# Attention in six half rounds a step, 256-column products between them, and sigmoids behind attention

## The chip, the cores and the metric

One core of a Trainium2 chip runs one program. The metric is the device time of one execution in microseconds; the median of three runs is quoted. TensorE (PE) multiplies, VectorE (DVE) and ScalarE (ACT) work on its results in PSUM banks of 512 f32 columns, GpSimd (POOL) works on SBUF, and SyncE (SP) issues most DMAs. Every engine runs its own instructions in their written order and waits on semaphores for the others.

## The reference

An AdaLN block on x (8 batch rows of 512 tokens, width 256), all in f32:

```python
mod = (_silu(c) @ wmod).reshape(8, 6, 1, -1)        # sa, ca, ga, sb, cb, gb; ga and gb kept away from 0
h = _layernorm(x) * (1 + ca) + sa
x = x + ga * attention(h)
h = _layernorm(x) * (1 + cb) + sb
x = x + gb * ffn(h)
```

`attention` has 16 heads over a latent of 64: `logits = q_lat @ latent_k / 8`, causal, softmax, times `latent_v`, up, then `Wout`. `ffn` is a mixture of 16 experts, each of which takes the 512 best of the 4096 tokens by `sigmoid(h @ gate_w.T)`, with gate, up and down products, plus a shared expert of width 512 (`silu(h @ shg) * (h @ shu)`, then `shd`) that all tokens pass.

## The kernel before

**Attention** goes in 32 steps; step n is batch row b and group g of four heads, `divmod(n, 4)`, written (b,g) here. In the body of the loop at L849 three steps overlap:

- For the next step, `scores` (L603) writes rows of query tile i against the keys that causality leaves (128(i+1) columns) into a bank `sc_ps`, and `maxima` (L611) reduces it on VectorE to the row maxima `mx`, one reduction with its accumulator's read for each head j and tile i.
- For this step, `fold` (L625) transposes the maxima on TensorE, and VectorE subtracts them from the query strips q (L630). Then `scores_t` (L632) writes the transposed scores of key tile c (512 - 128c columns) into a bank `st_ps`, and `exps` (L640) makes p on ScalarE; on every second head GpSimd masks the diagonal block (L650).
- For the last step, `context` (L660) multiplies v by p into `po`, 16 matmuls of four tiles c; ScalarE copies it to `oT`, and `gather` sends it off by DMA. For every second step the sums' reciprocal (`invert`), a store and a fetch through DRAM (`fetch`) and a multiplication on VectorE (`divide`, L698) follow.

The 128 x 128 array holds sixteen 32 x 32 matmuls at once; `quarters` (L555) issues four for one head, so that two heads of the next step and two of this one fill it. This is a half round: all with the same number of columns, 512, 384, 256 or 128. A step has eight (k = 0 to 7), two of each size. Banks come from rotating tags: three for `sc_ps` (and fold's transposes), three for `st_ps`, and two, tag m, for everything else, context included.

Between half rounds stand the **slots**: `plan(n)` lists the other work of a step with a price in us of TensorE (0 for what others do), and `laid_out` deals it to nine slots by a table of VectorE's time for each half round. The other work: transposes, latents, queries, keys and values of rows to come (`turn_h` L483, `latents` L493, `query` L581, `key` L596, `value` L502), `residual` (L537) of the row before, the second norm and the gate's scores (`Second`), and the shared expert of the rows behind (`Shared`, L272; two rows within attention, "early", the others after it). A product of 512 columns with its two weight halves is two pieces of one matmul each. Written order of a step: slot 0, fold, context of tiles 0 and 1, half round 0, context of tiles 2 and 3, slot 1, half round 1, slot 2, and so on to slot 8.

`sigmoid` (L439) makes the gate's sigmoids of two batch rows by a polynomial on VectorE, in four parts, and stores them with two DMAs. Three of the four calls are in the plan of steps (3,0), (5,0) and (7,0), in slots 1, 3, 5 and 7.

**After attention** a tail (L900 to L921) ends the last row; after each of its parts `work()` issues two pieces of the late shared products. A search on VectorE (L967) finds each expert's threshold in 30 rounds, again with `work()` in between, and the experts follow, about half of the time, which the change does not touch.

Of the kernel before, what the change touches and what calls it, by code (L numbers as in the profile page):

```python
# [50 lines left out]
def block_kernel(ctx: ExitStack, tc: tile.TileContext, a: dict, out: bass.AP):  # L51
# [219 lines left out]

    class Shared:  # L272
# [10 lines left out]
        def product(self, ps, w, f, c):  # L283
            nc.tensor.matmul(
                ps,
                lhsT=w[:, c, f * P : (f + 1) * P],
                rhs=h2T[:, c, self.b * T : (self.b + 1) * T],
                start=(c == 0),
                stop=(c == KC - 1),
            )  # L290

        def gate(self, f, c):
            if c == 0:
                if f == 0:
                    flush()
                    self.begin()
                self.pg = bank("pg2") if self.early else bank_s("pg2")
            self.product(self.pg, shg, f, c)
            if c < KC - 1:
                return  # L300
# [8 lines left out]
        def up(self, f, c):  # L309
            if c == 0:  # L310
                self.pu = bank("pu2") if self.early else bank_t("pu2")
            self.product(self.pu, shu, f, c)
            if c < KC - 1:
                return
# [7 lines left out]
        def down(self, i, h):  # L322
            i2, ii = divmod(i, 2)
            if h == 0:
# [3 lines left out]
            for f in range(h * NS // 2, (h + 1) * NS // 2):  # L328
                nc.tensor.matmul(
                    self.py[:, ii, :],  # L330
                    lhsT=self.mid[:, f, i * P : (i + 1) * P],
                    rhs=shd[:, f, :],
                    start=(f == 0),
                    stop=(f == NS - 1),
                )
            if ii == 1 and h == 1:
# [18 lines left out]
        def units(self):  # L355

            for f in range(NS):
                for c in range(KC):
                    yield c == 0, lambda f=f, c=c: self.gate(f, c)
                for c in range(KC):  # L360
                    yield c == 0, lambda f=f, c=c: self.up(f, c)
            for i in range(TT):
                for h in range(2):
                    yield i % 2 == 0 or h == 0, lambda i=i, h=h: self.down(i, h)
# [103 lines left out]
    class Row:  # L468
# [24 lines left out]
        def latents(self, cs=range(KC)):  # L493
            for c in cs:
                if c == 0:
                    self.lat = ap.tile([P, T], F32, name="lat", bufs=1)
                    self.pl = bank("pl")
                nc.tensor.matmul(self.pl, lhsT=wkv[:, c, :], rhs=self.hT[:, c, :], start=(c == 0), stop=(c == KC - 1))
                if c == KC - 1:
                    nc.scalar.copy(self.lat, self.pl)  # L500

        def value(self, i2):  # L502
            pv = bank("pv").rearrange("p (i h w) -> p i h w", h=H, w=DH)
            for ii in range(2):
                i = 2 * i2 + ii
                nc.tensor.matmul(
                    pv[:, ii, :, :].rearrange("p h w -> p (h w)"),
# [5 lines left out]
            for ii in range(2):  # L513
                nc.scalar.copy(v[:, 2 * i2 + ii, :, 0:HS:2], pv[:, ii, :, :])
# [22 lines left out]
        def residual(self, i):  # L537
            i2, ii = divmod(i, 2)
            if ii == 0:
                self.py = bank("py").rearrange("p (i d) -> p i d", d=D)  # L540
            for c in range(KC):
# [7 lines left out]
            if ii == 1:  # L549
# [10 lines left out]
    class Step:  # L560
# [20 lines left out]
        def query(self, cs=range(KC)):  # L581

            for c in cs:
                if c == 0:
                    self.pq = bank("pq")
                nc.tensor.matmul(
                    self.pq,
                    lhsT=wq[:, c, self.g * P // 2 : (self.g + 2) * P // 2],
                    rhs=self.r.hT[:, c, :],
# [3 lines left out]
                if c == KC - 1:  # L593
                    self.spread(self.pq, "q8", q_strips)

        def key(self):  # L596
            pk = bank("pk")
            nc.tensor.matmul(
                pk, lhsT=wlat[0:L, self.g * P // 2 : (self.g + 2) * P // 2], rhs=self.r.lat[0:L, :], start=True, stop=True
            )  # L600
            self.spread(pk, "k8", k_strips)

        def scores(self, j, i):  # L603

            n = (i + 1) * P
            sc_ps = bank_t("sc_ps") if self.n == 0 and j % 2 else bank_s("sc_ps")
            k = self.strip(j)
            quarters(sc_ps[:, 0:n], self.q[k, i * P : (i + 1) * P], self.k[k, 0:n])
            return sc_ps

        def maxima(self, sc_ps, j, i):  # L611
# [3 lines left out]
                sc_ps[:, 0:n],  # L615
                sc_ps[:, 0:n],
# [15 lines left out]
        def scores_t(self, j, c):  # L632

            n = T - c * P
            st_ps = bank_t("st_ps")
            k = self.strip(j)
            quarters(st_ps[:, 0:n], self.k[k, c * P : (c + 1) * P], self.q[k, c * P : T])
            return st_ps

        def exps(self, st_ps, j, c):  # L640
            n = T - c * P
            if c == 0 and j == 0:
                self.p = {}
            if j == 0:
                self.p[c] = ap.tile([P, NG, n], F32, name=f"p{c}", tag=f"p{c}", bufs=1)
            nc.scalar.activation(self.p[c][:, j, :], st_ps[:, 0:n], AF.Exp, scale=SCALE)  # L646
            if j % 2 == 1:
# [74 lines left out]
    SLOTS = 2 * TT + 1  # L722

    def plan(n):
# [4 lines left out]
        def add(slot, us, fn):  # L729
            todo.append((slot, us, fn))  # L730

        if n < 0:
            add(1, 1.8, modulate_t)
            for c in range(KC):
                add(2 + 2 * c, 0.86, lambda c=c: steps[2].query([c]))
            return todo
        if n == 0:
            for i in range(TT):
                add(i, 0.0, lambda i=i: stats(TT + i, mv))
# [4 lines left out]
        if g == (1 if b > 0 else 2) and b + 1 < B:  # L744
            for c in range(KC):
                add(0, 0.5, lambda c=c: rows[b + 1].turn_h(c))
            for c in range(KC):
                add(0, 0.86, lambda c=c: rows[b + 1].latents([c]))
        if n + 2 < len(steps) and n % 2 == 0:
            for c in range(KC):  # L750
# [616 lines left out]
```

## Time and profile before

| | us |
|---|---|
| median of 3 runs (1375.0 to 1378.51) | 1375.79 |
| the profiled execution | 1378.61 |
| its span, first to last instruction | 1376.9 |
| first fold to last fold (31 steps of attention) | 30.95 to 552.34 |
| last step and tail | 552.34 to 621.03 |
| search, placing, first fetch | 621.03 to 708 |
| experts | 708 to 1376.9 |

In the lines of the profile, times are us from the span's start unless marked ns; "x" is a count of records. A matmul in f32 is two records, each with a weight load (PEld). A matmul's end is modelled, and matmuls are pipelined, so the distance from one start to the next tells more than a length. What stands in brackets is the engine's idle time ahead of the instruction and whoever ended it. A row of a table by stretch has the stretch, its length, each engine's busy time, the granted TensorE clock as a share of full speed, and the DMA engines' share and rate. A slot's work is known by its line: L284 shared gate and up, L329 shared down, L488 `turn_h`, L498 latents, L506 values, L542 residual, L586 queries, L598 keys, L398 `turn`.

### The profile page before, as it was taken

The numbers are of one execution on the slowest core, as the hardware profiler recorded it, in microseconds if no ns is written. First come the engines' busy times: TensorE is split into PE (matmuls) and PEld (weight loads), VectorE is DVE, ScalarE is ACT, GpSimd is POOL, SyncE is SP. The second block draws the span as 40 slices with busy tenths as digits, with TensorE's granted clock in tenths as the row PEclk, the third lists the DMA queues.
The fourth block names the chain that finished last, engine by engine and source line by source line (L and its number), as shares of the span: only waits on it lengthen the run. The fifth ranks groups of instructions, "written<-read, shape, count | busy, mean of one in ns | idle before, by whom it ended". The sixth has DMA issues, their size and how long they took to land. (4 is left out here: it accounts for less than half of the span.)

```text
span 1376.9 us, 34203 instructions
## 1 busy us (share of the span) xinstructions
PE 1334.4 (97%) x14002; PEld 864.3 (63%) x14002; DVE 886.8 (64%) x2342; ACT 483.7 (35%) x1125; POOL 544.5 (40%) x629
## 2 busy tenths in 40 slices
PE   9999999989999899999999999999999999999997
PEld 4444334434434334465555888888888888888885
DVE  5756567656665667246664767777676777777653
ACT  1655555555455454411111322223332222333221
POOL 4552525252615232310013543454554345555331
PEclk9999999999999999999999999999999999999999
DMA  7122212221231221217022354444445444444511
GB/s 237 43 71 47 74 41 59 53 72 38 64 65 48 51 65 48 59 42 227 20 66 93 82 143 130 120 116 127 124 97 143 127 124 109 135 114 107 143 16 16
DMA packets 84349, 122.42 MB, mean 89 GB/s; under 512 B 14937, under 2 KB 61657, under 8 KB 84193
## 3 DMA queue, kind: packets, MB, share of 16 engines
q1 hardware_dynamic: 69120, 93.76, 22.7%
q0 software_dynamic: 14336, 25.70, 9.7%
q8 instruction: 110, 1.80, 0.5%
q10 hardware_dynamic: 736, 0.79, 0.2%
q14 instruction: 47, 0.38, 0.1%
HBM read 90.33 MB, written 21.51 MB: 81 GB/s over the span
## 5 line engine op out<-in xcount | busy, mean ns | idle before, releaser
L614 DVE CUSTOM_DVE_ANT_0 sc_ps<-sc_ps,causal 128x256 f32<-128x256 f32 (+3 forms) x512 | 240.9, 514 | 125.0 <-PE sc_ps L558 72.2
L646 ACT ACTIVATE p<-st_ps 128x256 f32<-128x256 f32 (+3 forms) x512 | 198.6, 439 | 212.1 <-PE st_ps L558 208.2
L558 PE MATMUL st_ps<-q,k 32*32 32x512 f32 (+3 forms) x4096 | 240.5, 443 | 2.4 <-ACT p L646 2.0
L558 PE MATMUL sc_ps<-k,q 32*32 32x512 f32 (+3 forms) x4096 | 236.8, 442 | 2.9 <-DMA k<-k 1.1
L1195 PE MATMUL epy<-dw,emid 128*128 128x256 f32 x1024 | 236.0, 382 | 1.8 <-DVE emid L1165 0.8
L650 POOL TENSOR_SCALAR_AFFINE_SELECT p<-p 128x256 f32<-128x256 f32 x256 | 105.2, 414 | 324.4 <-ACT p L646 323.5
L1220 POOL DMA_INDIRECT out<-eo,idx x64 | 102.1, 1596 | 315.9 <-DVE eo L1212 190.8
L1195 PEld LDWEIGHTS epy<-dw,emid 128*128 128x128 f32 x1024 | 192.0, 190 | 38.3 <-DVE emid L1165 12.9
L1142 ACT COPY c<-eu 128x256 f32<-128x256 f32 x120 | 44.7, 373 | 400.4 <-issue 224.9
L1125 PE MATMUL eu<-xsum,wsum 128*128 128x256 f32 x720 | 176.1, 381 | 0.0
L558 PEld LDWEIGHTS sc_ps<-k,q 32*32 32x32 f32 x4096 | 71.4, 103 | 142.4 <-DVE mx L614 89.2
L1125 PEld LDWEIGHTS eu<-xsum,wsum 128*128 128x128 f32 x720 | 135.7, 190 | 17.9
L1125 PE MATMUL eu<-xT,gu 128*128 128x256 f32 x480 | 142.8, 379 | 0.0
L1082 POOL DMA_INDIRECT rows<-rows_d,idx x64 | 62.3, 974 | 135.8 <-DVE mid L320 94.5
L1144 DVE TENSOR_TENSOR c<-eu,c 128x256 f32<-128x256 f32 x120 | 51.0, 425 | 100.8 <-ACT c L1143 98.4
L1165 DVE SCALAR_TENSOR_TENSOR emid<-eu,ub,esg 128x512 f32<-128x512 f32 x128 | 90.1, 743 | 28.8 <-ACT esg L1161 19.4
L1161 ACT ACTIVATE esg<-eu,gbias 128x512 f32<-128x512 f32 x128 | 81.5, 684 | 58.3 <-PE eu L1125 33.6
L1125 PEld LDWEIGHTS eu<-xT,gu 128*128 128x128 f32 x480 | 91.2, 190 | 12.4
L1145 DVE TENSOR_TENSOR eu<-eu,c 128x512 f32<-128x512 f32 x120 | 83.9, 699 | 4.1
L665 PE MATMUL po<-p,v 128*32 128x512 f32 (+3 forms) x1024 | 84.1, 447 | 0.6 <-DVE sg L305 0.5
L1042 DVE TENSOR_TENSOR at_q<-pos_lo,iota 128x1024 bf16<-128x1024 f32 x64 | 75.2, 1217 | 0.0
L614 DVE DVE_READ_ACCUMULATOR2_ANT mx<- 128x1 f32 x512 | 72.5, 142 | 0.0
(187 smaller groups left out, 1875.6 us busy)
## 6 DMA issues: line engine op xcount, KB each, us to landing
gu<-in_gw SPq DMA_DIRECT2D x16, 1024.0 KB
gu<-in_up SPq DMA_DIRECT2D x16, 1024.0 KB
dw<-in_dw SPq DMA_DIRECT2D x16, 1024.0 KB
q<-q SPq DMA_DIRECT2D x32, 128.0 KB
rows_d<-mod_d SPq DMA_DIRECT2D x8, 512.0 KB
rows_d<-row SPq DMA_DIRECT2D x8, 512.0 KB
out<-ysb SPq DMA_DIRECT2D x16, 256.0 KB
k<-k SPq DMA_DIRECT2D x30, 128.0 KB
```

Of the source, the lines that this page charges most:

```text
L558: nc.tensor.matmul(out[w : w + HS, :], lhsT=lhsT[:, w : w + HS], rhs=rhs, start=True, stop=True)
L614: nc.vector.tensor_tensor_reduce(sc_ps[:, 0:n], sc_ps[:, 0:n], causal[:, T - n : T], 1.0, -3.0e38, ALU.add, ALU.max, self.m[:, i, o : o + 1],)
L646: nc.scalar.activation(self.p[c][:, j, :], st_ps[:, 0:n], AF.Exp, scale=SCALE)
L650: nc.gpsimd.affine_select(out=p, in_=p, pattern=[[0, 2], [1, P]], compare_op=ALU.is_ge, fill=0.0, base=0, channel_multiplier=-1,)
L665: nc.tensor.matmul(self.po[self.strip(j), c * P : T], lhsT=v[:, c, self.g * NG + j, :], rhs=self.p[c][:, j, :], start=(c == 0), stop=(c == ...
L1042: nc.vector.tensor_tensor(self.at_q[:, n, :], pos_lo[:, e, n].unsqueeze(2).to_broadcast([P, QT, P]), iota.unsqueeze(1).to_broadcast([P, QT ...
L1125: nc.tensor.matmul(self.u[:, q, :], lhsT=w, rhs=x, start=start, stop=True, skip_group_check=not start)
L1145: nc.vector.tensor_tensor(u[:, 1:3, :], u[:, 1:3, :], c3.unsqueeze(1).to_broadcast([P, 2, HC]), ALU.add)
L1161: nc.scalar.activation(sg, pg, AF.Silu, bias=gbias[:, e, f : f + 1])
L1165: nc.vector.scalar_tensor_tensor(mid[:, f, :], pu, ub[:, e, f : f + 1], sg, ALU.add, ALU.mult)
L1195: nc.tensor.matmul(self.py[:, jj, :], lhsT=self.mid[:, f, j * P : (j + 1) * P], rhs=self.dw[:, f, :], start=(n == 0), stop=(n == NF - 1),)
L1220: nc.gpsimd.indirect_dma_start(out=out[:, :], out_offset=bass.IndirectOffsetOnAxis(ap=t.idx[:, j : j + 1], axis=0), in_=eo[:, jj, :], in_o ...
```

## The change

- A step has three rounds, six half rounds, seven slots. The last round holds query tiles 1 and 0 and key tiles 2 and 3: 256 columns and 128 columns side by side in one bank. Four reductions and two exps of 384 columns work on a pair of such banks, where four reductions and four exps did in two half rounds.
- The context of the last step stands whole at the head of the step, then fold, then slot 0. `invert`, `fetch` and `divide` stand after half rounds 2, 3 and 5 (before: 3, 5 and 7 of eight).
- Products are split into halves of 256 columns (`PARTS`); a piece is one such matmul, priced 0.44.
- `laid_out` deals pieces by what VectorE needs in a slot (a table, plus 0.5 for each `stats`) less what TensorE has of its own there, and the rest evenly. `turn` stands fixed in slot 0.
- The three sigmoid calls go into the tail, one of their twelve parts after each of the first twelve tail functions.

The diff, cut to its core; the products `product`, `gate`, `up`, `latents`, `query` and `key` are all split as `query` is, and `down` and `residual` into single matmuls:

```diff
+    PARTS = [(h, c) for h in range(2) for c in range(KC)]
+
+    def cols(h):
+        return slice(h * T // 2, (h + 1) * T // 2)
...
-        def query(self, cs=range(KC)):
-
-            for c in cs:
-                if c == 0:
+        def query(self, parts=PARTS):
+
+            for h, c in parts:
+                if (h, c) == PARTS[0]:
                     self.pq = bank("pq")
+                t = cols(h)
                 nc.tensor.matmul(
-                    self.pq,
+                    self.pq[:, t],
                     lhsT=wq[:, c, self.g * P // 2 : (self.g + 2) * P // 2],
-                    rhs=self.r.hT[:, c, :],
+                    rhs=self.r.hT[:, c, t],
...
-        def exps(self, st_ps, j, c):
-            n = T - c * P
-            if c == 0 and j == 0:
+        def exps(self, st_ps, j, cs, n):
+
+            if cs[0] == 0 and j == 0:
                 self.p = {}
             if j == 0:
-                self.p[c] = ap.tile([P, NG, n], F32, name=f"p{c}", tag=f"p{c}", bufs=1)
-            nc.scalar.activation(self.p[c][:, j, :], st_ps[:, 0:n], AF.Exp, scale=SCALE)
-            if j % 2 == 1:
+                p = ap.tile([P, NG, n], F32, name=f"p{cs[0]}", tag=f"p{cs[0]}", bufs=1)
+                for c, at in zip(cs, (0, T - cs[0] * P)):
+                    self.p[c] = p[:, :, at : at + T - c * P]
+                self.all = p
+            nc.scalar.activation(self.all[:, j, :], st_ps[:, 0:n], AF.Exp, scale=SCALE)
+            for c in cs:
+                if j % 2 == 0:
+                    continue
...
-    SLOTS = 2 * TT + 1
+
+    ROUNDS = [((TT - 1,), (0,)), ((TT - 2,), (1,)), ((1, 0), (2, 3))]
+    SLOTS = 2 * len(ROUNDS) + 1
...
-        def add(slot, us, fn):
-            todo.append((slot, us, fn))
+        def add(eighth, us, fn, dve=0.0):
+            todo.append((min(SLOTS - 1, int(eighth * (SLOTS - 1) / 8 + 0.5)), us, dve, fn))
...
-                add(i, 0.0, lambda i=i: stats((b - 1) * TT + i, mv2))
+                add(i, 0.0, lambda i=i: stats((b - 1) * TT + i, mv2), 0.5)
...
-                add(0, 0.5 * spread, lambda c=c: seconds[b - 1].turn(c))
+                add(0, 0.0, lambda c=c: seconds[b - 1].turn(c), -0.5)
...
-        if g == 0 and b % 2 == 1 and b > 1:
-            s = sigmoid(b - 3, 2)
-            for i in range(4):
-                add(2 * i + 1, 0.0, lambda: next(s))
...
-        k = 2 * SHARE[b][g]
+        k = 4 * SHARE[b][g]
...
-            add(2, 0.88, fn)
+            add(2, 0.44, fn)
...
-    DVE_US = (1.65, 1.65, 1.39, 1.39, 1.12, 1.12, 0.85, 0.85)
-    OWN_US = (0.5, 2.4, 0.9, 0.9, 0.9, 0.7, 0.7, 0.5, 0.5)
+    DVE_US = (1.0, 1.4, 1.4, 1.1, 1.1, 1.4, 1.4)
+    OWN_US = (1.2, 1.2, 1.0, 1.0, 1.1, 1.1, 3.0)
...
-        total = sum(us for _, us, _ in todo) + sum(OWN_US)
-        due = [1.4] + [d for d in DVE_US]
-        room, done, floor = [], 0.0, 0
-        for k in range(SLOTS):
-            room.append(total * sum(due[: k + 1]) / sum(due) - sum(OWN_US[: k + 1]))
+        need = [d - o for d, o in zip(DVE_US, OWN_US)]
...
+                need[s] += dve
+        need = [max(0.0, x) for x in need]
+        total, asked = sum(us for _, us, _, _ in todo), sum(need)
+        if total < asked:
+            need = [x * total / asked for x in need]
+        rest = max(0.0, total - asked) / SLOTS
+        room = [sum(need[: k + 1]) + rest * (k + 1) for k in range(SLOTS)]
...
-        fill(0)
+        if last is not None:
+            last.context(list(range(TT)))
         if now is not None:
             now.fold()
-        if last is not None:
-            last.context([0, 1])
-        for k in range(2 * TT):
-            c, half = divmod(k, 2)
-
+        fill(0)
+        for k in range(2 * len(ROUNDS)):
+            (tiles, cs), half = ROUNDS[k // 2], k % 2
+
+            sc_of, st_of = {}, {}
+            at_s = at_t = 0
+            for part, (i, c) in enumerate(zip(tiles, cs)):
+                for jj in range(2):
+                    if nxt is not None:
+                        j = 2 * (1 - half) + jj
+                        if part == 0:
+                            sc_of[j] = bank_t("sc_ps") if nxt.n == 0 and j % 2 else bank_s("sc_ps")
+                        nxt.scores(sc_of[j], j, i, at_s)
+                    if now is not None:
+                        j = 2 * half + jj
+                        if part == 0:
+                            st_of[j] = bank_t("st_ps")
+                        now.scores_t(st_of[j], j, c, at_t)
+                at_s += (i + 1) * P
+                at_t += T - c * P
             for jj in range(2):
                 if nxt is not None:
-                    j = 2 * (1 - half) + jj
-                    nxt.maxima(nxt.scores(j, TT - 1 - c), j, TT - 1 - c)
+                    j, at = 2 * (1 - half) + jj, at_s
+
+                    for i in reversed(tiles):
+                        at -= (i + 1) * P
+                        nxt.maxima(sc_of[j], j, i, at)
                 if now is not None:
                     j = 2 * half + jj
-                    now.exps(now.scores_t(j, c), j, c)
-            if last is not None and k == 0:
-                last.context([2, 3])
...
+                    now.exps(st_of[j], j, cs, at_t)
...
                 if last.g % 2 == 1:
+                    if k == 2:
+                        last.invert()
                     if k == 3:
-                        last.invert()
+                        last.fetch()
                     if k == 5:
-                        last.fetch()
-                    if k == 7:
                         last.divide()
...
+    sigmoids = chain.from_iterable(sigmoid(b, 2) for b in range(0, B - 2, 2))
     for fn in tail:
         fn()
+        next(sigmoids, None)
         work()
```

`work()` issues four of the smaller pieces instead of two. In the changed kernel the lines move: `turn_h` is L494, the queries L596, the fold's transposes L645, its subtraction L646, the maxima L630.

## The prediction

> **What bounds the kernel now.** I read the page's first part, then the busy time by stretch, then the timelines of TensorE and VectorE through single steps, then the waits.
>
> ```profile
> PE 1334.4 (97%) x14002; PEld 864.3 (63%) x14002; DVE 886.8 (64%) x2342; ACT 483.7 (35%) x1125; POOL 544.5 (40%) x629
> ```
>
> No other engine is near TensorE. But its share counts pipelined matmuls, so I look at starts. By stretch (us, then busy us of each engine, then granted clock):
>
> ```profile
> core 0: us, PE busy (x) PEld busy (x) DVE busy (x) ACT busy (x) POOL busy (x), PEclk, DMA share, GB/s
> 288.08:308.33 20.25, 17.05 (x316) 7.77 (x317) 10.13 (x36) 9.75 (x24) 10.70 (x16) 0.97 0.37 102
> 308.33:325.95 17.62, 17.62 (x316) 7.71 (x316) 11.61 (x44) 7.99 (x19) 3.27 (x8) 0.94 0.12 24
> ...
> 171.93:188.51 16.58, 16.58 (x317) 7.30 (x315) 11.60 (x44) 7.99 (x19) 3.27 (x8) 1.00 0.14 27
> ```
>
> Each row is one attention step, fold to fold: steps (4,0), (4,1), (2,1) by batch row and group. The 31 steps from 30.95 to 552.34 take 521.4 us; the tail, the search and the experts follow. Now TensorE inside a step (start, length, form):
>
> ```profile
> 294.38 0.53 PE L558 MATMUL sc_ps<-k,q 32*32 32x384 f32 x4
> ...
> 295.24 0.69 PE L598 MATMUL pk<-lat,wlat 64*128 64x512 f32 x1
> ...
> 296.30 0.53 PE L558 MATMUL sc_ps<-k,q 32*32 32x384 f32 x4
> ...
> 297.00 0.60 PE L558 MATMUL sc_ps<-k,q 32*32 32x256 f32 x5
> ...
> 298.58 1.13 PE L506 MATMUL pv<-wlat,lat 64*128 64x256 f32 x4
> 299.64 0.42 PE L558 MATMUL sc_ps<-k,q 32*32 32x256 f32 x4
> ...
> 300.28 1.12 PE L284 MATMUL pu<-h2T,shu 128*128 128x512 f32 x2
> 301.34 0.31 PE L558 MATMUL sc_ps<-k,q 32*32 32x128 f32 x4
> ```
>
> A half round is 32 such records. One of 384 columns takes 0.86 us to a following product (294.38 to 295.24) and 0.70 to a following half round (296.30 to 297.00); 128 columns with a half round behind take 0.32. A product pair takes 1.06 between half rounds (300.28 to 301.34), 0.86 among other products:
>
> ```profile
> 187.65 1.02 PE L586 MATMUL pq<-hT,wq 128*128 128x512 f32 x2
> 188.51 0.27 PE L629 MATMUL pmx<-ident,mx 128*128 128x128 f32 x1
> ```
>
> So one excursion out of the scores and back costs 0.16 + 0.20 = 0.36 us. The half round at 297.00 needed 0.64 and took 1.58: it waited for a bank that VectorE was still reducing. Over the 31 steps (who waited for whom: us, times, longest):
>
> ```profile
> PEld sc_ps L558 <- DVE mx L614: 87.4, 189, 1.2
> ```
>
> That is the weight loads' row; what TensorE loses is counted below. The other kind of wait is at the end of step (4,0):
>
> ```profile
> 306.08 0.69 DVE L698 TENSOR_TENSOR hd<-hd,one 128x512 f32<-128x512 f32 x1 [2.99 <-DMA one<-one_d]
> 306.69 0.68 DVE L317 SCALAR_TENSOR_TENSOR mid<-sg,pu 128x512 f32<-128x512 f32 x1
> ```
> ```profile
> 303.62 0.60 PE L488 MATMUL pt<-ident,xn 128*128 128x128 f32 x4
> 307.42 1.11 PE L488 MATMUL pt<-ident,xn 128*128 128x128 f32 x4 [3.20 <-DVE mid L317]
> ```
>
> The division waits for its DMA, the product's evacuation queues behind it, and TensorE's transposes queue behind that for a bank. The next row of stretches shows clock 0.94: fold and context there ran 1.0 us long.
>
> I took each segment's spacing less the spacing of its form without a wait. Over the 31 steps TensorE works 446.5 us and waits 75: 38.4 on half rounds of 256 and 128 columns, 15.3 on 384, 2.7 on 512, 13.2 on products behind a bank, 5.3 fold and context at the low clock. The waits are 59.5 us in batch rows 1 to 6 (9.9 a row), 12.2 in row 0, 3.2 in row 7.
>
> **The change part by part.**
>
> *Merged half rounds.* Four short half rounds of a step become two of 256 + 128 columns. That is the 384-column form: 0.70, against 0.48 (0.64 less 0.16) + 0.32 = 0.80. Two a step, 31 steps: 0.2 x 31 = **6.2 us** less. VectorE keeps its four reductions a pair; by start-to-start spacings (0.22 for 128, 0.39 for 256, last read 0.14) a merged half round holds it 1.4 us, as one of 512 does (1.41). ScalarE does one exp of 384 (0.496) for 387 + 278 ns; it waits for TensorE anyway: nothing.
>
> *Pieces.* In the compiled order the scores are left 180 times in the 31 steps before and 156 times after: 24 x 0.36 = **8.6 us** less. The split itself costs nothing by the rows: the residual's 256-column products run four records in 1.06 between half rounds (180.89 to 181.95), just as two of 512. [...]
>
> *Waits in rows 1 to 6*, from the order after, per row. Without a product between them, two half rounds lie apart by VectorE's way back: start 0.1 after TensorE, first reduction and read 0.62 + 0.14, release 0.06, then the remaining scores 0.7 to 0.9; TensorE idles 0.9 (after 512) or 0.8 (after 384 or merged). Step (b,0) has 0.5 to 0.9 us of products in every slot: 0.5 left for the reciprocal and other VectorE work. (b,1): 0.2. (b,2): one empty slot, 0.8. (b,3): two, 1.7. At the step's start the context now comes before the fold, so the subtraction on q (0.1 + 0.69 + 0.1) is covered only by slot 0, 0.43 to 0.93 of products: 0.4 each in (b,1) and (b,2). The context itself needs the last masks: exps 0.2 + 2 x 0.5, selects 0.1 + 2 x 0.41, so 2.1 us after the scores; the step's last slot (0.43 or more) and its own first two tiles (0.88 + 0.76, from 172.46 to 174.10) cover that. ScalarE's copy of the context (0.59) now stands ahead of the first half round's exps; ScalarE is busy 8 to 10 us of a step, so nothing. The division: on SP's queue its store and fetch now go behind both spreads of q and k in (b,2) and around the one of k in (b,0), which wait for products done two slots earlier. From reciprocal to landed DMA it took 5.9 to 8 us before (0.4, then 1.4 to 3.5 to the fetch's issue, then 4), and three half rounds lie between, 5.6 us; it waits some 1.6, but context and fold (2.9) now stand between it and the transposes that stalled 3.2. I take 0.7 each in (b,0) and (b,2), where 0 and 2 are the ends. Behind it on VectorE stand one evacuation and the subtraction, for which the next scores wait. Sum 0.5 + 0.2 + 0.8 + 1.7 + 0.8 + 1.4 + 0.2 (rounding) = 5.6 against 9.9: 4.3 x 6 = 26; I take **23.5**, since VectorE's stats may come in a bad place. Ends: 0 (waits only move) and 43 (they fall to 2.8 a row).
>
> *The clock.* The low clock follows the long waits, so its 5.3 us go with them (inside the 23.5). [...]
>
> *Rows 0 and 7:* steps (0,1), (0,3), (7,2) have almost no products and are set by the way to VectorE and back: some 12.8 against 13; 0.
>
> *Last step:* two warm-up products fewer, 2 x 0.63, and closer rounds: **1.5 us** less.
>
> *Sigmoids.* Three groups, 16.3 us of VectorE by their rows, leave steps (3,0), (5,0), (7,0). (3,0) took 17.78, (2,0) without one 18.16, so their leaving gains nothing. In the tail (552.34 to 621.03) TensorE works 68.4 of 68.7 us at the shared products and VectorE 23.5: hidden, 0. Uncovered they would cost 16.3. Their six small DMAs (0.44 us of issue each) pass on SP's queue ahead of the expert weights: 2.6 us there, 60 us before the gather needs anything.
>
> Sum: 6.2 + 8.6 + 23.5 + 1.5 = 39.8. The profiled execution took 1378.61 (span 1376.9), so 1338.8 for one like it; the median of the runs, 1375.79, is 2.8 lower: **1336 us**.
>
> **The rivals.** The compiled order has merged rounds and pieces where the change puts them, so that it does nothing is none of them. *Waits only move* (the division's stall reappears before the subtraction, VectorE's work in the wrong slots): 16.3 remain, 1359.5. For: every step's VectorE has 10 to 13 us of work in 15. Against: slots without a product fall to three in a row of four steps.
> *Waits go further*: half of the 5.6 too, 1319. For: step (2,1) shows a step with 0.6 of wait.
> *The boundary goes serial* (slower): context at the step's start waits for exps and selects, 2.1, and the subtraction adds 0.9, with nothing beside: 3.0 less the 0.4 counted = 2.6 x 31 = 80, so 1416. It decides from 1.3 us a step on (39.8 / 31). Against: the context waits tile by tile, and its first two tiles are long ready. For: before, half a context and a whole half round stood there as cover.
> *Weight loads show* (slower): the split adds 192 products, 384 loads of 190 ns, 73 us if none was hidden: 1409 with all else gained. Against: eight records of 256 columns take 1.73 in the tail, four of 512 take 1.72. [...]
>
> **How the numbers follow.** Forecast (1322 to 1352) 0.58; waits only move 0.17; waits go further 0.12; serial boundary 0.11; loads 0.02. The range, 1314 to 1364, holds the forecast's, some 0.12 of the waits that only move and 0.08 of those that go further; the slow cases are left out. A measurement tells some 0.3%, 4 us. Faster 0.84, same 0.04, slower 0.12.
>
> **What would show it.** Right: steps (b,0) and (b,2) of 15 to 16 us, no transposes at L494 waiting over 1 us, clock 1.0 through attention, merged half rounds 0.70 apart, the tail's TensorE still full. Wrong: context rows waiting for POOL, scores waiting for q's subtraction over 0.5 us a step, or a tail over 69 us.

## The result, and the profile after

The change made the kernel faster: 1360.66 us (median of 4 runs, 1358.32 to 1362.49) against 1377.15 (4 runs beside them), ratio 0.9878, interval 0.9849 to 0.9907. That is 16.5 us, less than half of the 39.8 of the sum, and the time of the first rival, in which waits only move (1359.5). It lies inside the range. But the table below shows that the rival's mechanism is not what happened: rows 1 to 6, where its waits should have stayed, lost 27.4 us, so that the two times meet by chance. The profiled execution went from 1378.61 to 1362.43.

By stretch, in the two profiled executions, against the sum (the 14.8 us of merged rounds and excursions dealt evenly over 31 steps, and the 23.5 of the waits on rows 1 to 6):

| us | before | after | forecast | measured |
|---|---|---|---|---|
| start to first fold | 30.95 | 37.51 | 0 | +6.6 |
| batch row 0 | 55.8 | 56.3 | -1.9 | +0.5 |
| rows 1 to 6 | 414.8 | 387.4 | -35.0 | -27.4 |
| row 7, three steps | 50.84 | 55.78 | -1.4 | +4.9 |
| last step and all behind it | 824.6 | 823.8 | -1.5 | -0.8 |

The first part of the page of after, then steps (4,0), (4,1), (3,1) and (7,0), fold to fold, by stretch (length, then each engine's busy time, granted clock, DMA):

```profile
PE 1330.9 (98%) x14382; PEld 940.4 (69%) x14382; DVE 896.8 (66%) x2342; ACT 469.3 (34%) x997; POOL 540.8 (40%) x629
```
```profile
286.00:302.64 16.64, 16.00 (x325) 7.94 (x321) 10.45 (x36) 8.49 (x19) 9.88 (x15) 1.00 0.55 127
302.64:319.41 16.77, 16.77 (x328) 8.97 (x324) 11.89 (x43) 8.28 (x16) 3.17 (x8) 1.00 0.13 23
238.57:255.38 16.81, 16.81 (x329) 9.01 (x325) 11.89 (x43) 8.28 (x16) 3.17 (x8) 1.00 0.12 22
481.14:503.75 22.61, 21.45 (x333) 10.60 (x329) 11.05 (x37) 9.04 (x20) 5.16 (x11) 0.85 0.49 102
```

Step (4,0), the one with the long stall, fell from 20.25 to 16.64, (4,1) from 17.62 to 16.8; (3,1), which like (2,1) took 16.58 and was almost without waits before, rose to 16.81. Rows 2, 3 and 5 now repeat to 0.02 us: 16.63, 16.80, 16.15, 14.44. But (7,0) rose from 19.59 to 22.6, with the clock at 0.85.

The wait of the weight loads on VectorE's reductions, 87.4 us before in the same 31 steps, and what TensorE's transposes of the next row wait for (the line, then us and times by releaser):

```profile
PEld sc_ps L567 <- DVE mx L630: 25.0, 61, 0.8
```
```profile
L494 PE MATMUL pt<-ident,xn x64: 272/273/475, 11.4 to 433.8; 128*128 128x128 f32 x64
...
  ACT hT L495: 5.0, 6
  DVE xn L485: 1.4, 5
```

The same line of before had this in its answer, the stall behind the division:

```profile
  DVE mid L317: 16.7, 6
```

Both moved as forecast. TensorE's time in rows 1 to 6, from start to start by what started, shows where the rest is:

| us, rows 1 to 6 | before | after | eight half rounds (E2) |
|---|---|---|---|
| half rounds of 512 | 53.2 | 60.8 | 65.2 |
| of 384 | 51.4 | 44.5 | 49.6 |
| of 256 and 128, merged or not | 77.9 | 68.1 | 66.1 |
| products, fold, context | 232.3 | 214.1 | 219.2 |
| times that the scores are left | 148 | 127 | 164 |

### The profile page after: what moved, and what is told of

Same layout as the page of the kernel before. It is cut to its first block, busy times and chain, and to the rows that moved or that the text cites. A ratio compares the mean times of both kernels' runs of the same rounds, so it can differ in the third digit from the quotient of the medians.

```text
span 1360.7 us, 34621 instructions
## 1 busy us (share of the span) xinstructions
PE 1330.9 (98%) x14382; PEld 940.4 (69%) x14382; DVE 896.8 (66%) x2342; ACT 469.3 (34%) x997; POOL 540.8 (40%) x629
## 5 line engine op out<-in xcount | busy, mean ns | idle before, releaser
L630 DVE CUSTOM_DVE_ANT_0 sc_ps<-sc_ps,causal 128x256 f32<-128x256 f32 (+3 forms) x512 | 245.5, 511 | 120.7 <-PE st_ps L567 65.0
L663 ACT ACTIVATE p<-st_ps 128x384 f32<-128x384 f32 (+1 forms) x384 | 181.5, 523 | 163.0 <-PE st_ps L567 133.1
L567 PE MATMUL st_ps<-q,k 32*32 32x512 f32 (+3 forms) x4096 | 229.6, 445 | 0.0
L669 POOL TENSOR_SCALAR_AFFINE_SELECT p<-p 128x256 f32<-128x256 f32 x256 | 101.7, 410 | 310.4 <-ACT p L663 309.8
L567 PEld LDWEIGHTS sc_ps<-k,q 32*32 32x32 f32 x4096 | 83.4, 104 | 94.5 <-issue 46.3
L684 PE MATMUL po<-p,v 128*32 128x256 f32 (+3 forms) x1024 | 77.5, 440 | 0.2 <-POOL p L669 0.2
L567 PEld LDWEIGHTS st_ps<-q,k 32*32 32x32 f32 x4096 | 69.7, 103 | 11.3 <-DVE q L646 5.8
```

The source lines that it names most:

```text
L567: nc.tensor.matmul(out[w : w + HS, :], lhsT=lhsT[:, w : w + HS], rhs=rhs, start=True, stop=True)
L630: nc.vector.tensor_tensor_reduce(sc_ps[:, at : at + n], sc_ps[:, at : at + n], causal[:, T - n : T], 1.0, -3.0e38, ALU.add, ALU.max, self. ...
L663: nc.scalar.activation(self.all[:, j, :], st_ps[:, 0:n], AF.Exp, scale=SCALE)
L669: nc.gpsimd.affine_select(out=p, in_=p, pattern=[[0, 2], [1, P]], compare_op=ALU.is_ge, fill=0.0, base=0, channel_multiplier=-1,)
L684: nc.tensor.matmul(self.po[self.strip(j), c * P : T], lhsT=v[:, c, self.g * NG + j, :], rhs=self.p[c][:, j, :], start=(c == 0), stop=(c == ...
```

## The experiments

All times are medians beside runs of the kernel before on the same chip (1376.7 to 1379.6); ratios compare best. A difference between two experiments comes out up to 3 us apart by the medians and by the ratios, so that a difference of that size settles nothing.

| | us | ratio to before |
|---|---|---|
| the change | 1360.7 | 0.9878 (0.9849 to 0.9907) |
| the change again (E11) | 1360.2 | 0.9859 (0.9834 to 0.9885) |
| E1 values' copies behind both products | 1350.3 | 0.9815 (0.9792 to 0.9838) |
| E5 E1, small products later | 1346.4 | 0.9765 (0.9743 to 0.9787) |
| E9 E5, more shared products in attention | 1368.3 | 0.9918 (0.9894 to 0.9942) |
| E12 E5, merged round of one width | 1364.2 | 0.9894 (0.9869 to 0.9920) |
| E2 eight half rounds | 1370.3 | 0.9966 (0.9944 to 0.9988) |
| E6 merged round bank by bank | 1370.8 | 0.9960 (0.9936 to 0.9983) |
| E4 old order at the boundary | 1378.2 | 1.0015 (0.9997 to 1.0032) |
| E8 before, new order at the boundary | 1378.7 | 0.9995 (0.9974 to 1.0015) |
| E10 old planner | 1374.2 | 0.9952 (0.9931 to 0.9973) |
| E7 pieces laid in twos | 1366.2 | 0.9906 (0.9886 to 0.9927) |
| E3 sigmoids back in attention | 1366.5 | 0.9935 (0.9916 to 0.9955) |

### A wait that the change adds: E1

In the trace after, the second value product of a pair starts late. TensorE's timeline in step (4,0), then the line's waits:

```profile
293.82 0.70 PE L516 MATMUL pv<-wlat,lat 64*128 64x256 f32 x2
295.15 0.70 PE L516 MATMUL pv<-wlat,lat 64*128 64x256 f32 x2 [0.64 <-ACT v L523]
```
```profile
294.70 0.40 ACT L523 COPY v<-pv 128x256 f32<-128x256 f32 x1
```
```profile
L516 PE MATMUL pv<-wlat,lat x64: 376/480/792, 41.6 to 490.8; 64*128 64x256 f32 x64
...
  ACT v L523: 12.3, 16
```

Splitting `value` put ScalarE's copy of the first half ahead of the second half's product. Both touch one bank, so the product waits for the copy (294.70 to 295.10), which queues behind two exps (293.94 to 294.81).

```diff
-                nc.scalar.copy(v[:, i, :, 0:HS:2], self.pv[:, ii, :, :])
+            if iis[-1] == 1:
+                for ii in range(2):
+                    nc.scalar.copy(v[:, 2 * i2 + ii, :, 0:HS:2], self.pv[:, ii, :, :])
```

> The changed kernel with one edit: the two copies of a bank of values are issued after both of its products, as before, not each after its own. Theory A (the second value product waits for ScalarE's copy of the first, since both touch one bank): the four records of the second value pair take 1.06 us again instead of 1.96 in step (b,0) of rows 2 to 6 and 2.52 in row 7: 5 x 0.9 + 1.5 + 1.0 in the first pair of row 7 = 7 us less, 10 if the stretch at half clock in step (7,0) (490.3 to 497.2) goes too: 1351 to 1354 where the changed kernel takes 1360.7. Rival B (the wait only moves, since VectorE sets these slots): step (b,0) keeps its 16.6 us and the time is within 2 us of the changed kernel.

Measured 1350.3, just under the band of theory A, whose signs it shows. The four records are one run again, steps (b,0) of rows 2 to 6 take 15.74 instead of 16.64, and (7,0) 17.47 instead of 22.6, at full clock:

```profile
290.22 1.13 PE L516 MATMUL pv<-wlat,lat 64*128 64x256 f32 x4
```
```profile
476.45:493.92 17.47, 17.47 (x333) 9.33 (x329) 11.05 (x37) 8.86 (x20) 5.13 (x11) 1.00 0.47 122
```

In (7,0) after, the two waits of the pairs (0.44 and 0.72 us idle) left TensorE busy for 2.37 of 3.40 us, and behind that stretch the clock halved:

```profile
487.05:490.45 3.40, 2.37 (x37) 1.01 (x38) 1.56 (x7) 2.29 (x6) 0.81 (x2) 0.98 0.57 128
490.45:497.25 6.80, 6.80 (x82) 2.96 (x88) 1.14 (x4) 1.26 (x3) 1.10 (x2) 0.51 0.50 116
```

The two products and their copies have different columns of the bank; that the program waits by bank and not by columns is what the 12.3 us show.

### The start: E5 and E11

In the profiled execution after, the clock is at half (0.50) from 26.35 to 43.35 us; before, it was at 1.00 there.

```diff
-            add(1, 1.8, modulate_t)
+            add(3, 1.8, modulate_t)
```

> The kernel with both copies of the values after both products, and one more edit: the second modulation's small products (16 records of 8 columns, 1.9 us) stand after two half rounds of the first scores instead of after one. Theory A (TensorE's clock halves at 26 to 27 us because the stretch of 3.4 us ahead holds little work, half a half round and those small products, and the thin first step keeps it low for 17 to 21 us, in all four kernels with six half rounds but not in the one with eight): first fold at 31 to 32 us instead of 36.1, step (0,0) about 14 instead of 16.7, so 7 us less than 1350.3: 1342 to 1345. Rival B (where the clock falls is chance): within 3 us of 1350.

> The changed kernel itself again, beside the two others on one chip. Theory A (where TensorE's clock falls is mostly chance): 1358 to 1363 again, steps of rows 2 to 5 the same to 0.05 us, but the first fold anywhere from 31 to 38 us and step (7,0) from 17 to 22.6 by where the half clock lies. Rival B (the order of this kernel brings both on): first fold at 36 to 38 us and (7,0) above 20 again.

E5 took 1346.4, between its theories, and its profiled execution did not do what theory A says: first fold at 36.08, half clock from 28.9 to 42.5. The 3.40 us ahead of the half clock held 67 records of TensorE in E5 (25.50 to 28.90) and 49 in the changed kernel (22.95 to 26.35), and TensorE was busy for all 3.40 in both; the kernel before has 63 from 23.80 to 27.20, also busy for all of it, and the clock is at 1.00 behind them. That little work ahead is the cause is not shown. E5's other runs were granted 0.992 to 0.997 over the whole, E1's 0.989 to 0.993, and the median fell by 3.9 (6.9 by the ratios). E9 has E5's order of TensorE up to step (1,3), and there the first fold came at 32.11. The same stretch in E5 and E9:

```profile
28.90:42.50 13.60, 12.32 (x143) 4.72 (x141) 8.01 (x33) 1.67 (x3) 0.41 (x1) 0.50 0.81 261
```
```profile
26.35:33.15 6.80, 5.38 (x112) 2.90 (x106) 6.02 (x30) 0.59 (x1) 0.00 (x0) 1.00 1.10 342
33.15:42.50 9.35, 9.35 (x139) 2.56 (x138) 6.58 (x21) 4.10 (x9) 1.09 (x3) 0.63 0.60 193
```

E11 is the changed kernel once more and repeats its picture, as rival B has it: first fold at 37.76, (7,0) 22.65, rows 2, 3 and 5 equal to 0.02. Over all profiled executions the first fold came at 35.1 to 38.4 in the nine that have the small products after one half round, and at 30.95, 31.9, 32.1, 36.1 and 37.6 in the five that have them after two. So the order seems to make the half clock likely, and the rest is chance; that rests on one profile of each kernel, and which stretch decides it is not settled.

### What a merged half round costs: E2, E6, E12

The prediction priced it as the 384-column form, 0.86 us between products. Between products it stands alone in 46 places; it takes 1.21 to 1.23 in 41 of them and never less. TensorE's timeline in step (3,1), one merged half round between two residual products:

```profile
247.48 1.13 PE L551 MATMUL py<-wo,hd 128*128 128x256 f32 x4
248.54 0.42 PE L567 MATMUL sc_ps<-k,q 32*32 32x256 f32 x4
...
249.00 0.52 PE L567 MATMUL sc_ps<-k,q 32*32 32x128 f32 x5
249.24 0.34 PE L567 MATMUL st_ps<-q,k 32*32 32x128 f32 x4
...
249.51 0.32 PE L567 MATMUL st_ps<-q,k 32*32 32x128 f32 x4
249.75 1.56 PE L551 MATMUL py<-wo,hd 128*128 128x256 f32 x6
```

Taken singly, 32 records of 256 columns start by 248.88, sixteen at a time 7 ns apart; the 33rd record starts at 249.00, the 34th only at 249.185, and from there one each 16.7 ns in a stream.

```diff
-    ROUNDS = [((TT - 1,), (0,)), ((TT - 2,), (1,)), ((1, 0), (2, 3))]
+    ROUNDS = [((TT - 1,), (0,)), ((TT - 2,), (1,)), ((1,), (2,)), ((0,), (3,))]
```

The planner's tables and the places of the division follow the eight half rounds.

> The changed kernel with eight half rounds of one token tile each instead of six; all else stays (context ahead of the fold, 256-column pieces, the new planner with the VectorE times 0.8 and 0.45 us for the short half rounds, sigmoids in the tail). Theory A (a merged half round has 64 records and takes 1.21 us whatever stands beside it, 0.35 more than a 384-column one of 32 records; apart, with a product between them, its two parts take 0.64 + 0.43, of which 0.36 is the switch that both pay): up to 0.14 x 62 = 9 us less than the changed kernel where products are there to stand between, 0 where there are none, so 1352 to 1361. Rival B (the prediction's sum: merged rounds save 6.2 us and fewer excursions up to 8.6): 1367 to 1376.

E2 came 9.7 us slower than the change (12 by the ratios), in rival B's band. Theory A had the prices right and the sum wrong: the table by form shows the short half rounds no dearer apart (66.1) than merged (68.1), but the scores are left 37 times more, which costs the products 5.1, and nine slots share what seven had, so the 512s and 384s wait 9.5 more. Merging pays through the slots, not through its own time.

E6 fills one bank with both widths before the next begins:

```diff
+            for jj in range(2):
+                at_s = at_t = 0
                 for part, (i, c) in enumerate(zip(tiles, cs)):
-                    for jj in range(2):
```

> The changed kernel with one edit: in a merged half round each score bank gets its 256 and then its 128 columns before the next bank begins, so the width changes three times in 64 records, not once. Three readings of the 1.21 us that a merged half round takes between products, where 0.86 had been forecast. Theory R (records: after the first 33 since the last product there is one gap of 0.185 us and then 16.7 ns a record): one gap again, 1.15 to 1.25 us, total within 4 us of the changed kernel's 1360.7. Theory S (each change of width costs 0.185): three gaps, 1.5 to 1.6 us, 15 to 23 us slower in all. Theory V (a hidden wait on VectorE): its first bank is ready earlier, under 1.1 us, 5 to 10 us faster.

Measured 1370.8, and 1.51 us a round in 46 places of 46: theory S by the round, though the total of 10.1 more is under its 15 to 23; V is out. Then E12, made from E5, with one width; the narrow tile of a merged round is also written first, so that what the reductions and the exp read stays together:

```diff
-            n = (i + 1) * P
+            n = max(i + 1, 2) * P
...
-            n = T - c * P
+            n = max(T - c * P, 2 * P)
```

> The kernel with both copies of the values after both products and the later small products (1346.4), and one edit: in a merged half round the narrow tile is computed 256 columns wide too (its outer 128 columns are never read), so that the 64 records have one width; the reductions and the exp read what they read before. More columns, no change of width. Theory S (a change of width inside the round costs some 0.15 us and slows the 128-column records after it): a merged half round between products takes 1.05 to 1.10 us, as one of 512 columns does, instead of 1.21; 0.11 to 0.16 x 62 = 7 to 10 us less, 1336 to 1340. Theory R (64 records cost what they cost, whatever their width): 1.21 or more, 1345 to 1355.

E12's round is theory R's, 1.42 us; its total, 17.8 us above E5, lies beyond R's band (0.21 us for 62 rounds is 13 of it). The timeline shows the pause in the same place, with no change of width near it:

```profile
250.46 0.42 PE L569 MATMUL sc_ps<-k,q 32*32 32x256 f32 x4
...
250.92 0.62 PE L569 MATMUL sc_ps<-k,q 32*32 32x256 f32 x5
251.16 0.45 PE L569 MATMUL st_ps<-q,k 32*32 32x256 f32 x4
...
251.88 1.56 PE L553 MATMUL py<-wo,hd 128*128 128x256 f32 x6
```

The 33rd record starts 0.46 after the first, the 34th 0.65, the rest at 16.7 ns. So S falls. The traces of both kernels say so too: in a run of two half rounds of 384 columns (before, at 194.75) the 34th record starts 0.166 us behind the 33rd, in one of two of 512 (after, at 208.96) 0.167, and no width changes there. E6 needs another reason. Its 34th record starts 0.64 us after the first, as in the change; what it loses lies behind, where the last of the 64 starts at 1.31 instead of 1.01. Its records start eight at a time instead of sixteen, since bank by bank only two heads' strips of the array work together; that this is the reason is argued from the starts, not tried by itself. What makes the pause behind the 33rd is not shown.

### The order at the boundary and the planner: E4, E8, E10

```diff
-        if last is not None:
-            last.context(list(range(TT)))
+        fill(0)
         if now is not None:
             now.fold()
-        fill(0)
+        if last is not None:
+            last.context([0, 1])
...
+            if last is not None and k == 0:
+                last.context([2, 3])
```

> The changed kernel with the old order at the step's boundary: slot 0, then the fold, then two of the four context tiles, and the other two after the first half round. Theory A (the new order is worth little either way: it saves one excursion of 0.36 us a step, 11 us in all, and leaves the subtraction on q uncovered, 0.4 us in steps (b,1) and (b,2) and 0.9 in (b,3), 11 us in all, and takes away the cover of the first half round's reductions): 1355 to 1367. Rival B (the new order is where the gain came from, since the division no longer holds the transposes of the next row): 1372 to 1380, with step (b,0) at 17.5 us or more.

E4 is rival B by its time: 17.5 us slower, all that the change had gained. Its sign, (b,0) at 17.5 us or more, came in rows 2, 6 and 7, not in rows 3 to 5 (16.5), and it is not the division: transposes at L494 wait 2.9 us on the product's evacuation, not 16.7. It is the fold. What TensorE's fold waited for, after and E4:

```profile
  DVE mx L630: 3.2, 3
```
```profile
  DVE mx L630: 19.6, 50
```

With the context ahead of the fold, its 2.3 us of matmuls cover VectorE's last reductions; with seven slots and the fold first only the products of two slots do, in (2,2) 1.1 us of them (194.96 to 196.06). Steps (b,2) of rows 2 to 6 took 17.7 to 18.2 instead of 16.15 (row 4: 16.76). E4 keeps the planner's table of the change, which still counts context and fold as work behind the last slot; how much of the loss is due to that is not tried.

E8 puts the new order alone into the kernel before (the last two lines are the planner's table):

```diff
-        fill(0)
+        if last is not None:
+            last.context(list(range(TT)))
         if now is not None:
             now.fold()
-        if last is not None:
-            last.context([0, 1])
+        fill(0)
...
-            if last is not None and k == 0:
-                last.context([2, 3])
...
-    OWN_US = (0.5, 2.4, 0.9, 0.9, 0.9, 0.7, 0.7, 0.5, 0.5)
+    OWN_US = (1.1, 1.1, 0.9, 0.9, 0.7, 0.7, 0.5, 0.5, 2.9)
```

> The kernel before with the new order at the step's boundary alone: all four context tiles, the fold, then slot 0; its planner gets TensorE's own work moved likewise. Eight half rounds, 512-column pieces, the old planner and the sigmoids in attention stay. Theory A (the order by itself takes most of the gain, 17.5 us as the changed kernel lost without it): 1355 to 1364. Rival B (it gains only with pieces and planner that fill slot 0 and the last slots): 1370 to 1380.

Rival B by its time: nothing gained. In the profiled execution, though, rows 1 to 6 took 403.0 us, 11.8 less than before. The division's stall is gone there too, but its last half rounds stand without products between (256 and 128 together 85.1 us in rows 1 to 6 for 77.9, 512s 60.1 for 53.2). The first fold came 6.6 us later and rows 0 and 7 took 4.9 more; up to the last fold the clock was at half for 41 us, against 27 before. So the order shortens rows 1 to 6 even alone, and part of that goes to the lower clock (the median granted to E8's runs is 0.9815, to those of before beside them 0.9875); why the clock is lower is open.

E10 takes the old rule of the planner, with its VectorE table cut to seven slots:

```diff
-        need = [d - o for d, o in zip(DVE_US, OWN_US)]
...
-        room = [sum(need[: k + 1]) + rest * (k + 1) for k in range(SLOTS)]
+        total = sum(us for _, us, _, _ in todo) + sum(OWN_US)
+        room = [total * sum(DVE_US[: k + 1]) / sum(DVE_US) - sum(OWN_US[: k + 1]) for k in range(SLOTS)]
```

> The changed kernel with the rule of the planner before: room up to a slot goes by the whole of TensorE's work in proportion to VectorE's share, and what VectorE has beside the reductions is not counted; 256-column pieces, six half rounds and the new boundary stay. Theory A (the new boundary pays only with a planner that fills the slots ahead of the context, as eight half rounds with the old planner gained nothing from it): 1368 to 1378, with empty last slots and the context waiting for POOL's masks. Rival B (pieces and merged rounds are enough; where they are laid is second): within 4 us of 1360.7.

E10's time is theory A's, its place isn't: the fold waits 5.2 us on maxima and the context 5.3 on POOL's masks, less than the changed kernel's 9.0. It took 14 us more than E11 on the same chip, 7.0 in the profiled executions. Two steps there are 11.8 us longer, (2,1) and (3,1), 22.8 and 22.6 us, where TensorE stands still for 3.1 and 4.3 us at the step's start; in (2,1) the profile names no releaser, and the granted clock is 0.50 from 176.80 to 182.75. Steps (4,1) and (5,1) take 17.67, so it is not shown that the planner's rule makes these waits. Why they come is left open.

### Pieces, sigmoids, empty slots: E7, E3, E9

```diff
-                for c in range(KC):
-                    add(0, 0.44, lambda i=i, c=c: rows[b - 1].residual(i, [c]))
+                add(0, 0.88, lambda i=i: rows[b - 1].residual(i))
```

and likewise for all other pieces.

> The changed kernel with the 256-column pieces laid in twos: every unit that the planner places is a pair, some 0.88 us as before the change; the matmuls stay 256 columns wide. Theory A (finer pieces are worth little: what they cover more evenly they pay for in excursions of 0.36 us): within 4 us of 1360.7. Rival B (the finer pieces are what lets a slot be filled to VectorE's work): some slots go empty at 0.9 us each, one more in most steps, 8 to 20 us slower.

E7 took 1366.2, 5.5 more (3.9 by the ratios, whose intervals overlap), between its theories: rows 1 to 6 4.1 longer, row 0 3.3, but rows 2, 3 and 5 only 0.4 to 0.6 each. The scores are left 118 times in rows 1 to 6 instead of 127, so more half rounds stand together without a product between. Finer pieces gain little by cover, and that they gain at all is not clear of the noise.

```diff
+        if g == 0 and b % 2 == 1 and b > 1:
+            sg = sigmoid(b - 3, 2)
+            for i in range(4):
+                add(2 * i + 1, 0.0, lambda: next(sg))
...
-        next(sigmoids, None)
```

> The changed kernel with the three groups of sigmoids back in attention, in the odd slots of steps (3,0), (5,0) and (7,0). Theory A (the prediction: their move to the tail is worth nothing, since TensorE sets those steps): 1361 plus 0 to 3. Rival B (VectorE sets the slots now, so its 16.3 us of sigmoids cost what they take): 1369 to 1377, with those three steps 3 to 5 us longer than 16.6.

E3 took 1366.5, 5.8 more (7.8 by the ratios), between its theories too. (5,0) grew by 1.1 at full clock, (3,0) by 3.8, the clock at half for part of it; what of the 5.8 is the sigmoids' own and what the clock's is not split:

```profile
223.16:243.64 20.48, 19.84 (x325) 9.26 (x321) 15.86 (x51) 9.47 (x20) 10.09 (x15) 0.83 0.35 92
```

VectorE is busy 15.86 us there, against 10.45 in (4,0) after.

```diff
-EARLY = 2
+EARLY = 3
-SHARE = [(0, 0, 0, 0), *[(1, 0, 1, 1)] * 6, (2, 2, 2, 0)]
+SHARE = [(0, 0, 0, 0), *[(1, 0, 2, 2)] * 6, (2, 2, 2, 2)]
```

> The kernel with both copies of the values after both products and the later small products (1346.4), and one edit more: the shared products of a third batch row are taken out of the tail into attention, four pieces of 256 columns more in steps (b,2) and (b,3) each (EARLY 3; shares 1, 0, 2, 2 and 2, 2, 2, 2 in row 7). Theory A (a slot without products costs 0.9 us of idle TensorE and there are one in (b,2) and two in (b,3), so 18 pairs cost 0.15 there instead of 0.86 in the tail, and the other 6 cost the same in both places): the tail 20.6 us shorter, attention 8 longer: 1332 to 1337. Rival B (VectorE sets those steps, so the 12 evacuations and the mids of the added products, some 10 us of VectorE, come on top): 1343 to 1350.

Both wrong: E9 took 1368.3, 21.9 more than E5; its profiled execution, the fastest of six, took 11.2 more. Rows 1 to 6 grew by 14.5 us in it, (2,3) from 14.44 to 15.75 for two more pairs, so a pair in an empty slot costs 0.65 and not 0.15. And what lies behind the last fold stayed at 825.4 (E5: 825.2). The tail and the search hand out their products at a fixed rate, so what was taken away is missing only at the end: the last shared product came 143.2 us after the last fold instead of 165.6, but the first expert's product at 165.1 (E5: 167.8), since the placing of the tokens takes its time anyway. TensorE was busy for 7.68 of 20.40 us there, at half clock:

```profile
685.10:705.50 20.40, 7.68 (x45) 4.34 (x46) 6.22 (x11) 1.17 (x2) 4.30 (x4) 0.50 0.23 66
```

## Why the time came out at less than half of the forecast

The step that failed is the price of a merged half round: it was taken from the 384-column form, 0.86 us between products, and takes 1.21. Two terms stood at nothing besides, the split of the values and the start. The waits, the largest term, were right.

**Waits in rows 1 to 6: right in kind and size.** By the prediction's own measure (spacing less that of the same form without a wait, 1.21 for a merged round) rows 2, 3 and 5 keep 5.1 us a row, 0.9 of it the new wait of the values, where 5.6 was forecast and 9.9 stood before. The division's stall went, step (b,2) takes 16.15, and an empty slot costs 0.8 (384, 256 and 128 columns in a row: 2.67, where 0.70 + 1.21 were needed) to 1.0 (two of 512: 2.96, where 0.91 + 1.07 were needed).

**What (b,0) should take** was 15 to 16 us; it took 16.64, and 15.74 without the values' wait. (b,2), for which the same was said, took 16.15.

**Merged half rounds: the term that was mis-sized.** "That is the 384-column form: 0.70": a form of 32 records was taken as the price of 64. Measured 1.21 between products instead of 0.86; over 62 of them that is 21.7 us above the forecast price. By the same measure TensorE's own work in rows 2, 3 and 5 is 58.9 us a row, where rows 1 to 6 had 59.2 before: 0.3 less, where the 14.8 of merged rounds and excursions come to 1.9. That merging still earns 9.7 by E2 comes from the slots, of which there are fewer to leave for and to fill, not from the round's own time. The sign "merged half rounds 0.70 apart" did not come. The pause behind the 33rd record could be read in the trace of before (0.166 us at 194.75); there its time went into the waits.

**Pieces: the step with no term.** "The split itself costs nothing by the rows" looked at products alone. The split of `value` also moves a copy, and behind it a wait: 10.3 us by E1's median, 8.7 by its ratio, and in the profiled executions 4.1 in rows 1 to 6 and 5.1 in row 7.

**The clock: wrong.** It was to follow the long waits and go with them. In the kernel before, half clock stood behind the waits of 3.20 and 2.39 us (0.53 from 307.30 to 310.75 and from 344.83 to 348.26), but behind the one of 3.25 at 448.50 the clock was at 1.00 (451.75 to 455.20), and in the 10 us ahead of the four other stretches of half clock up to the last fold TensorE was never idle for more than 0.43 us at a time. The changed kernel's profiled execution has half clock for 17 us at the start and 6.8 in (7,0); the table's +6.6 at the start is the largest miss outside the attention rows. (7,0) is explained by the values, the start only in part. In (7,0) the half clock (0.51 from 490.45 to 497.25) stood behind idle times of 0.44 and 0.72 us, far under the 3.2 of before.

**Sigmoids at 0: too low.** E3 says 5.8, with the clock's part in it; they fill slots of steps in which VectorE is then busy for 15.86 of 20.48 us (E3's (3,0)). That they are free in the tail holds: TensorE is busy 66.70 us of 69.58 ahead of the search's first count, which came 69.55 us after the last fold, 70.77 before.

**The boundary.** The slow rival's wait exists, 9.0 us of context on POOL's masks in 38 places, but 0.3 a step is far from the 1.3 where it decides. The subtraction on q adds 0.40 to a 512 half round (1.47 for 1.07), as forecast. What the prediction didn't see is the order's worth: it took away the fold's wait on the maxima, and in the time it shows only with the new slots (E4 and E8 both end at the time of before).

**The weight loads** do not show: four records of 256 columns still take 1.06 us between half rounds (247.48 to 248.54).

Of the 23.6 us that are missing in the profiled executions, 6.6 are at the start, 7.6 in rows 1 to 6 (the values' copies 4.1), 6.3 in row 7 (the values' 5.1), 2.4 in row 0 and 0.7 at the end. By six times rows 2, 3 and 5, an estimate, TensorE's own work fell there by 9.6 us less than the sum had it and the waits by 5.3 more than its 23.5. The rest is not split further by these runs. E1 and E5 beat both kernels: 1350.3 and 1346.4.

## What to carry to other kernels

When a product is split, follow its evacuation too: here a copy between two writes of one bank made the second product wait for ScalarE's queue, 0.9 us a time in steps (b,0) of rows 2 to 6. Price a group of small matmuls by its records as well as its columns, from a row with as many records in a run: here 32 of 384 columns took 0.86 us between products, and 64 of 256 and 128 took 1.21. An edit can show nothing in the time until another one stands beside it, as the order at the boundary did here, so undo edits one at a time before crediting any.

## What was not expected of the hardware

- After a product, 33 score records start within 0.46 us, the first 32 of them sixteen at a time 7 ns apart (the changed kernel at 248.54, E12 at 250.46); then comes a pause of 0.185 us in the one and 0.19 in the other, and a pace of 16.7 ns a record in a stream, with 128 columns in the changed kernel and 256 in E12.
- In the changed kernel half clock (0.50) lasted 17 us (26.35 to 43.35) while TensorE was busy for 15.73 of 17.00, for the most part in a stretch of scores for one step alone; the kernel before kept full clock (1.00) over the same 17 us, busy for 15.58.
